# A 7x7 depthwise convolution on one core: two image rows to a partition at loading, odd rows moved by ScalarE

## The chip, the core and the metric

One core of a Trainium2 chip runs the whole program. Its engines work side by side, each through its own queue in order: TensorE (PE in the profile; PEld is its weight load), VectorE (DVE), ScalarE (ACT), GpSimd (POOL) and SyncE (SP), which here only issues DMA transfers. SP and ACT both issue DMAs. Engines and DMAs wait for each other through semaphores. The metric is the device time of one execution in microseconds (us); lower is better. Before the change the median of 14 runs is 9291.06 us (9283.38 to 9296.27).

## What is computed

Two layers work on a tensor x of 32 images, 128 channels and 56 x 56 pixels, all in float32. The first is a depthwise 7x7 convolution, then a layer norm, a mixture of experts and a residual sum; the second is a per-token attention and a second, softly routed mixture. The change touches only the convolution:

```python
def _forward(input, dw_kernel, dw_bias, ...):      # input: (32, 128, 56, 56)
    x = jax.lax.conv_general_dilated(
        input, dw_kernel, (1, 1), ((3, 3), (3, 3)),
        feature_group_count=C, dimension_numbers=('NCHW', 'OIHW', 'NCHW')
    ) + dw_bias[None, :, None, None]
    x = jnp.transpose(x, (0, 2, 3, 1))             # layer norm, router, experts follow
    ...
```

So every channel has its own 7x7 filter, and each of its 32 images is filtered with a border of three zeros.

## The kernel before

The convolution runs as matmuls over image rows. A loop of 64 steps (`for c in range(CH)`) treats two channels at once: channel c on partitions 0 to 63, the "half" r = 0, and channel c + 64 on partitions 64 to 127, the half r = 1. Image row h of a channel lies on partition r*64 + h, so 56 of each half's 64 partitions are used. A partition holds that row of all 32 images, each with three zeros on both sides (`xin`, 32 x 62 numbers). The filter enters as a band matrix (`band`, one DMA per half), which DVE turns over into `br` with its output columns sorted into even and odd rows (L265); a POOL instruction (L269) adds some bands. `xs` (L273, POOL) holds the sums of neighbouring pixels.

`products(c, part)` (L226 to L249) makes three kinds of products: part 0, "evens", from every other pixel of `xin` with 4 taps; part 1, "odds", the same with 3 taps; part 2, "boths", from `xs` with 4 taps. For each tap and each half it issues four matmuls, one for each pair of 16 images (b) and row parity (i). The four lie on four column strips of the PE array, and the half chooses the rows of the array, as `tile_position=(r * HP, q)` says. I call these four a block. One step has 8 + 6 + 8 = 22 blocks, 88 matmuls; a float32 matmul leaves two records in the profile, so a step has 176. The text issues the blocks of the two halves in turn.

After the products, for each half r: ACT copies the evens from PSUM to `ea` (L281); DVE makes the even pixels of the result (`ot`, L285, twice), then evens out of boths (L289), then the odd pixels (L294, twice); ACT issues two DMAs that write `ot` to `conv_d` (L299). `xin`, `band` and `br` have three buffers each, filled in turn; the PSUM pool has eight banks, of which a step takes six.

What a reader sees as one loop is spread over the queues by a scheduler when the program is built: it places each instruction on its engine's queue by what it takes to be the earliest time, so that the queue order is not the order of the text. In the program before, the blocks of the halves alternate through all 64 steps, and ACT's queue runs, from step 1 on, in pairs of steps: `ea` of two steps (four copies), then the eight write DMAs of the two. Each DMA also takes one of eight semaphores in rotation, and waits until the DMA that had it last has landed.

After the loop a router stage begins with small constants (`gam`, `wg`, `bet`, `bgt`, `raw`, `jm`, `jl`) and the reading back of `conv_d` (`ct`). In the program before, the loads of `gam`, `wg` and `bgt` and most work on `raw`, `jm` and `jl` stand early in the convolution.

Of the kernel before, what the change touches and what calls it, by code (L numbers as in the profile page):

```python
# [8 lines left out]
F32 = mybir.dt.float32  # L9
# [3 lines left out]
ALU = mybir.AluOpType  # L13
# [4 lines left out]
P = 128  # L18
GJ = 7
GT = P * GJ  # L20
KS = 7
PAD = 3
# [3 lines left out]
def conv_attn_hybrid_kernel(  # L26
# [24 lines left out]
    nc = tc.nc  # L51
    N, C, H, W = x.shape
# [34 lines left out]
    band_d = dram.tile([C, KS * 2 * H], F32, name="band_d")  # L87
# [106 lines left out]
    WP = W + 2 * PAD  # L194
    HP = P // 2
    NB = N // 2
    WH, CH = W // 2, C // 2
    NE, NO = (KS + 1) // 2, KS // 2
    BL = (KS - 1) * 2 * H + H
    HH, QP = H // 2, P // 4  # L200
    assert H <= HP and N % 2 == 0 and W % 2 == 0 and NB * (WH + 1) * 4 <= 2048
    assert H % 2 == 0 and HH <= QP
    with tc.tile_pool(name="cv_c", bufs=1) as cc, tc.tile_pool(
        name="cv", bufs=3
    ) as cv, tc.tile_pool(name="cv_p", bufs=8, space=PSUM) as cvp:
        wt = cc.tile([C, KS, KS], F32, name="wt")
        nc.sync.dma_start(wt.rearrange("c a b -> c (a b)"), dw_kernel.rearrange("c o a b -> c (o a b)"))
        gp = cc.tile([C, KS, 2 * H], F32, name="gp")
        nc.vector.memset(gp, 0.0)
        for kh in range(KS):  # L210
            nc.vector.tensor_copy(gp[:, :, H - 1 - PAD + kh], wt[:, kh, :])
        nc.sync.dma_start(band_d, gp.rearrange("c a b -> c (a b)"))
        bias = cc.tile([P, C], F32, name="bias")
        nc.sync.dma_start(bias, dw_bias.partition_broadcast(P))

        nbuf = 3
        bands = [cc.tile([P, KS, 2 * H], F32, name=f"band{i}") for i in range(nbuf)]
        turned_bands = [cc.tile([P, KS + NO, 2, QP], F32, name=f"br{i}") for i in range(nbuf)]
        xins = [cc.tile([P, N, WP], F32, name=f"xin{i}") for i in range(nbuf)]
        for i in range(nbuf):  # L220
            nc.vector.memset(bands[i], 0.0)
            nc.vector.memset(turned_bands[i], 0.0)
            nc.gpsimd.memset(xins[i], 0.0)
        cview = conv_d.rearrange("n c (h w) -> c h n w", w=2 * W)

        def products(c, part):  # L226

            bt, xi, xs = turned_bands[c % nbuf], xins[c % nbuf], sums_of_x[c]
            wide = WH + (part == 1)
            pss = [cvp.tile([P, NB, wide], F32, name="cps") for r in range(2)]  # L230
            taps = NO if part == 1 else NE
            for a in range(taps):
                for r in range(2):
                    rows = slice(r * HP, r * HP + H)
                    for b in range(2):
                        imgs = slice(b * NB, (b + 1) * NB)
                        if part < 2:
                            at_ = 2 * a + part
                            w_, m_ = at_, xi[rows, imgs, at_ : at_ + 2 * wide - 1 : 2]
                        else:  # L240
                            w_, m_ = (0, KS, KS + 1, KS + 2)[a], xs[rows, imgs, a : a + WH]
                        for i in range(2):
                            q = i * HP + b * QP
                            nc.tensor.matmul(  # L244
                                pss[r][q : q + QP], bt[rows, w_, i, :], m_,
                                start=(a == 0), stop=(a == taps - 1),
                                tile_position=(r * HP, q), skip_group_check=True,
                            )
            return pss  # L249

        sums_of_x = {}
        for c in range(CH):
            bt, br, xi = bands[c % nbuf], turned_bands[c % nbuf], xins[c % nbuf]
            for r in range(2):
                rows, cr = slice(r * HP, r * HP + H), r * CH + c
                nc.sync.dma_start(
                    bt[rows].rearrange("p a b -> p (a b)")[:, :BL],
                    bass.AP(
                        band_d.tensor, band_d.offset + cr * KS * 2 * H, [[1, H], [1, BL]]
                    ),  # L260
                )
                nc.sync.dma_start(
                    xi[rows, :, PAD : PAD + W], x[:, cr].rearrange("n h w -> h n w")
                )
            nc.vector.tensor_copy(  # L265
                br[:, :KS, :, :HH],
                bt[:, :, :H][:, :, ::-1].rearrange("p k (h i) -> p k i h", i=2),
            )
            nc.gpsimd.tensor_tensor(  # L269
                br[:, KS:, :, :HH], br[:, 2:KS:2, :, :HH], br[:, 1 : KS - 1 : 2, :, :HH], ALU.add  # L270
            )
            xs = sums_of_x[c] = cv.tile([P, N, WP // 2], F32, name="xs")
            nc.gpsimd.tensor_tensor(xs, xi[:, :, 0::2], xi[:, :, 1::2], ALU.add)  # L273
            evens = products(c, 0)
            odds = products(c, 1)
            boths = products(c, 2)
            ot = cv.tile([P, NB, 2, W], F32, name="ot", bufs=3)
            for r in range(2):
                cr = r * CH + c
                ea = cv.tile([P, NB, WH], F32, name="ea", bufs=4)  # L280
                nc.scalar.copy(ea, evens[r])  # L281
                mine = slice(r * HP, (r + 1) * HP)
                for i in range(2):
                    of = slice(i * HP, (i + 1) * HP)
                    nc.vector.scalar_tensor_tensor(  # L285
                        ot[mine, :, i, 0::2], odds[r][of, :, :WH], bias[of, cr : cr + 1], ea[of],
                        ALU.add, ALU.add,
                    )
                nc.vector.scalar_tensor_tensor(  # L289
                    ea, boths[r], bias[:, cr : cr + 1], ea, ALU.add, ALU.subtract  # L290
                )
                for i in range(2):
                    of = slice(i * HP, (i + 1) * HP)
                    nc.vector.tensor_tensor(  # L294
                        ot[mine, :, i, 1::2], ea[of], odds[r][of, :, 1:], ALU.subtract
                    )
                for b in range(2):
                    q = r * HP + b * QP
                    nc.scalar.dma_start(  # L299
                        cview[cr][:, b * NB : (b + 1) * NB, :],  # L300
                        ot[q : q + HH].rearrange("p n i w -> p n (i w)"),
                    )
# [96 lines left out]
    with tc.tile_pool(name="rt_c", bufs=1) as cc, tc.tile_pool(  # L399
        name="rt", bufs=6  # L400
# [170 lines left out]
        loaded, c = 0, 0  # L571
# [16 lines left out]
    with tc.tile_pool(name="sel", bufs=1) as se, tc.tile_pool(  # L588
        name="sel2", bufs=2
# [260 lines left out]
    with tc.tile_pool(name="sc_c", bufs=1) as cc, tc.tile_pool(  # L850
        name="sc", bufs=4
# [181 lines left out]
    with tc.tile_pool(name="ex_w", bufs=2) as ew, tc.tile_pool(  # L1033
        name="ex", bufs=3
# [72 lines left out]
        for i, (e, b) in enumerate(blocks):  # L1107
            n = GR if b < NBIG else GR // NQ
# [112 lines left out]
    with tc.tile_pool(name="at_c", bufs=1) as cc, tc.tile_pool(  # L1221
        name="at", bufs=2
# [524 lines left out]
        while k < NT or work or choosing or choices:  # L1747
# [15 lines left out]
            if k == NT // 2 + 3:  # L1763
                rows = at.tile([E2, FF2], F32, name="hbr", tag="zr", bufs=1)
# [16 lines left out]
    with tc.tile_pool(name="f_c", bufs=1) as cc, tc.tile_pool(  # L1781
        name="f", bufs=2
    ) as fp, tc.tile_pool(name="f_p", bufs=1, space=PSUM) as fps, tc.tile_pool(
        name="o", bufs=2
# [21 lines left out]
        for i in range(NS):  # L1806
# [11 lines left out]
            h = fp.tile([P, FF2], F32, name="fh")  # L1818
# [107 lines left out]
```

## Time and profile before

| | us |
|---|---|
| median of 14 runs | 9291.06 |
| the profiled execution, whole | 9286.61 |
| its span (first to last instruction) | 9284.9 |
| first matmul of the convolution | 12.96 |
| end of its last matmuls | 600.2 |
| PE busy in 100 to 600 us | 499.3 of 500 |
| ACT busy in 100 to 600 us | 55.3 of 500 |

The span is what one execution shows between its first and last instruction; the whole time has 1.7 us more around it. Rows of a timeline give the start, the time and the engine, then the source line, the operation, what is written and read, and how many instructions were merged into the row; in brackets stands the idle time before the first of them and what ended it. Here 56*32 beside a matmul is the part of the array it uses, and 56x448 the moving operand. A busy share close to 1 on PE does not show by itself that PE sets the pace, since the ends of its matmuls are modelled.

### The profile page before, as it was taken

The numbers are of one execution on the slowest core, as the hardware profiler recorded it, in microseconds if no ns is written. First come the engines' busy times: TensorE is split into PE (matmuls) and PEld (weight loads), VectorE is DVE, ScalarE is ACT, GpSimd is POOL, SyncE is SP. The second block draws the span as 40 slices with busy tenths as digits, with TensorE's granted clock in tenths as the row PEclk, the third lists the DMA queues.
The fourth block names the chain that finished last, engine by engine and source line by source line (L and its number), as shares of the span: only waits on it lengthen the run. The fifth ranks groups of instructions, "written<-read, shape, count | busy, mean of one in ns | idle before, by whom it ended". The sixth has DMA issues, their size and how long they took to land. (4 is left out here: it accounts for less than half of the span.)

```text
span 9284.9 us, 169079 instructions
## 1 busy us (share of the span) xinstructions
PE 8369.2 (90%) x64986; PEld 6988.8 (75%) x64986; DVE 6611.2 (71%) x9050; ACT 5297.9 (57%) x13301; POOL 7025.1 (76%) x4996
## 2 busy tenths in 40 slices
PE   9996667776999999996999999999999999999988
PEld 5776455554777777775889999999999999999744
DVE  7879766675222222225999999999999999999623
ACT  1138322232333333334888888888888888888600
POOL 2235466665888888888999999999999999999500
PEclk9998788888999999998999999999999999999855
DMA  9984255564444444442000000000000000000299
GB/s 205 219 212 151 84 161 170 172 176 142 74 73 74 68 73 71 68 71 32 25 31 29 32 32 32 25 32 32 29 32 32 25 32 32 29 31 32 87 313 328
DMA packets 865534, 828.22 MB, mean 89 GB/s; under 512 B 403162, under 2 KB 756829, under 8 KB 845628
## 3 DMA queue, kind: packets, MB, share of 16 engines
q1 hardware_dynamic: 457818, 472.35, 18.0%
q0 software_dynamic: 177664, 188.81, 11.5%
q10 hardware_dynamic: 229248, 156.26, 5.7%
q8 instruction: 515, 8.44, 0.4%
q14 instruction: 289, 2.37, 0.1%
HBM read 464.45 MB, written 353.64 MB: 88 GB/s over the span
## 5 line engine op out<-in xcount | busy, mean ns | idle before, releaser
L161 POOL TENSOR_TENSOR s<-s,q 128x2048 f32<-128x2048 f32 x784 | 3600.7, 4610 | 54.8 <-DVE s L161 30.3
L161 DVE TENSOR_TENSOR s<-kv,c 128x2048 f32<-128x2048 f32 x784 | 1787.1, 2279 | 22.3 <-POOL c L161 19.9
L161 POOL DMA_INDIRECT t_d<-ys,xe x992 | 1543.1, 1556 | 330.3 <-issue 285.2
L161 DVE TENSOR_TENSOR ev<-s,kv 128x2048 f32<-128x2048 f32 x784 | 1783.6, 2275 | 1.0 <-ACT s L161 1.0
L161 ACT ACTIVATE s<-s 128x2048 f32<-128x2048 f32 x784 | 1506.0, 1921 | 467.7 <-POOL s L161 464.2
L161 PE MATMUL sm<-ident,s 128*128 128x128 f32 x12544 | 1521.6, 275 | 72.8 <-DVE oT L161 65.1
L161 PE MATMUL sm<-ident,ev 128*128 128x128 f32 x12544 | 1518.5, 275 | 1.8 <-DVE ev L161 1.8
L161 PEld LDWEIGHTS sm<-ident,s 128*128 128x128 f32 x12544 | 1395.6, 142 | 95.3 <-issue 74.8
L161 PEld LDWEIGHTS sm<-ident,ev 128*128 128x128 f32 x12544 | 1427.3, 143 | 46.7 <-DVE ev L161 3.8
L1132 ACT ACTIVATE hT<-ph,b1t 128x512 f32<-128x512 f32 (+1 forms) x992 | 680.1, 686 | 1128.1 <-PE ph L161 1120.6
L1149 DVE TENSOR_TENSOR ys<-py,b2t 128x512 f32<-128x512 f32 (+1 forms) x248 | 171.5, 692 | 1400.5 <-PE py L161 1304.3
L863 POOL DMA_INDIRECT xb_d<-xs,rd x784 | 768.9, 981 | 484.0 <-issue 205.7
L161 PEld LDWEIGHTS py<-w,hT 128*128 128x128 f32 x7936 | 924.1, 191 | 116.9 <-issue 64.0
L161 PE MATMUL py<-w,hT 128*128 128x128 f32 x7936 | 925.3, 275 | 0.0
L161 PE MATMUL ph<-xeT,w 128*128 128x512 f32 (+1 forms) x1984 | 905.6, 600 | 0.0
L161 PEld LDWEIGHTS ph<-xeT,w 128*128 128x128 f32 x1984 | 364.8, 194 | 363.3 <-issue 359.7
L161 ACT COPY add<-px 128x512 f32<-128x512 f32 x224 | 116.1, 533 | 843.2 <-remote 514.6
L161 DVE SCALAR_TENSOR_TENSOR xs<-pa,rst,add 128x256 f32<-128x256 f32 x784 | 331.2, 478 | 338.7 <-remote 108.8
L161 PE MATMUL pa<-rw,ct 128*128 128x256 f32 x1568 | 410.3, 411 | 142.8 <-DVE xs L161 88.2
L161 PEld LDWEIGHTS pa<-rw,ct 128*128 128x128 f32 x1568 | 323.7, 210 | 266.5 <-issue 139.1
L161 PE MATMUL kv<-wq,zT 128*128 128x256 f32 x1568 | 418.0, 390 | 57.5 <-DVE ev L161 57.4
L244 PE MATMUL cps<-xin,br 56*32 56x448 f32 (+1 forms) x7168 | 441.0, 584 | 16.5 <-DVE br L265 13.0
(354 smaller groups left out, 13779.7 us busy)
## 6 DMA issues: line engine op xcount, KB each, us to landing
ct<-conv_d SPq DMA_DIRECT2D x192, 448.0 KB
xin<-in_x_dram SPq DMA_DIRECT2D x128, 392.0 KB
conv_d<-ot ACTq DMA_DIRECT2D x256, 196.0 KB
t_d<-xs ACTq DMA_DIRECT2D x112, 448.0 KB
tr<-t_d SPq DMA_DIRECT2D x112, 448.0 KB
out_dram<-oo ACTq DMA_DIRECT2D x32, 1568.0 KB
to<-t_d SPq DMA_DIRECT2D x30, 1568.0 KB
xg<-in_x_dram SPq DMA_DIRECT2D x96, 448.0 KB
```

The costliest lines, as they stand in the source:

```text
L161: r = getattr(self.engine, name)(*a, **k)
L244: nc.tensor.matmul(pss[r][q : q + QP], bt[rows, w_, i, :], m_, start=(a == 0), stop=(a == taps - 1), tile_position=(r * HP, q), skip_group ...
L863: s = nc.gpsimd.indirect_dma_start(out=xb_d, out_offset=bass.IndirectOffsetOnAxis(ap=idx, axis=0), in_=row, in_offset=None, bounds_check=R ...
L1132: nc.scalar.activation(hT[:, f, :, :rows], ph[:, :, :rows], AF.Gelu, bias=b1t[:, f : f + 1])
L1149: nc.vector.tensor_tensor(ys[:rows], py[:rows], across(b2t, SB)[:rows], ALU.add)
```

## The change

The shape of the load changes. Two consecutive image rows of a channel are contiguous in DRAM, so that one descriptor can carry 112 numbers instead of 56. Row pair p of a half now arrives on partition r*64 + p (28 partitions, 448 bytes a piece); ACT then copies the second row of each pair to partition r*64 + 32 + p, so that even image rows lie on partitions 0 to 27 of a half and odd rows on 32 to 59. `xin` grows from 32 x 62 to 32 x 118 numbers on a partition, as the odd row needs a place beside the even one. The load overwrites the right border, so POOL clears it again in every step (new L274). The band matrix is split alike, even and odd rows by a DMA each: four band DMAs in a step where there were two. The matmuls take all 64 partitions of a half, with zeros in the unused ones. Line numbers after L250 move by up to ten.

```diff
-        xins = [cc.tile([P, N, WP], F32, name=f"xin{i}") for i in range(nbuf)]
+        xins = [cc.tile([P, N, WP + W], F32, name=f"xin{i}") for i in range(nbuf)]
...
-                    rows = slice(r * HP, r * HP + H)
+                    rows = slice(r * HP, (r + 1) * HP)
...
             for r in range(2):
-                rows, cr = slice(r * HP, r * HP + H), r * CH + c
+                cr = r * CH + c
+                for i in range(2):
+                    q = r * HP + i * QP
+                    nc.sync.dma_start(
+                        bt[q : q + HH].rearrange("p a b -> p (a b)")[:, :BL],
+                        bass.AP(
+                            band_d.tensor, band_d.offset + cr * KS * 2 * H + i,
+                            [[2, HH], [1, BL]],
+                        ),
+                    )
+                q = r * HP
                 nc.sync.dma_start(
-                    bt[rows].rearrange("p a b -> p (a b)")[:, :BL],
-                    bass.AP(
-                        band_d.tensor, band_d.offset + cr * KS * 2 * H, [[1, H], [1, BL]]
-                    ),
-                )
-                nc.sync.dma_start(
-                    xi[rows, :, PAD : PAD + W], x[:, cr].rearrange("n h w -> h n w")
-                )
+                    xi[q : q + HH, :, PAD : PAD + 2 * W],
+                    x[:, cr].rearrange("n (h i) w -> h n (i w)", i=2),
+                )
+                nc.scalar.copy(
+                    xi[q + QP : q + QP + HH, :, PAD : PAD + W],
+                    xi[q : q + HH, :, PAD + W : PAD + 2 * W],
+                )
+            nc.gpsimd.memset(xi[:, :, PAD + W : WP], 0.0)
...
-            nc.gpsimd.tensor_tensor(xs, xi[:, :, 0::2], xi[:, :, 1::2], ALU.add)
+            nc.gpsimd.tensor_tensor(xs, xi[:, :, 0:WP:2], xi[:, :, 1:WP:2], ALU.add)
```

The scheduler also builds other queues from this text. What stands in them is part of the program as built:

- ACT, from step 5 on in most steps: `ea` of step c (two copies), the copy of half 1 of step c+1, the copy of half 0 of step c+2, the four write DMAs of step c. At steps 28, 34, 40, 46, 52 and 58 it is `ea`, then both halves of c+1 and half 0 of c+2.
- PE: the evens of 40 of the 64 steps (1, 6 to 26, 30 to 32, 36 to 38, 42 to 44, 48 to 50, 54 to 56, 60 to 62) no longer alternate. Three blocks of half 0 stand in a row, then three of half 1, then the fourth of each, which waits for POOL's clearing. Odds and boths alternate as before, and so do the evens of the other 24 steps.
- SP: two band DMAs more in each step, and the loads of `gam`, `wg`, `bgt` and `bet` stand behind the convolution; so does the work on `raw`, `jm` and `jl`.

## The prediction

> **What bounds the kernel now.** I read the stage table first (busy time by 100 us), then the weight loads of single steps, then who waits in 100 to 560 us, then ACT and DVE at the stage's end.
>
> ```profile
> 100.00:200.00 100.00, 100.00 (x1972) 65.79 (x1964) 83.41 (x128) 10.53 (x21) 26.19 (x22) 1.00 1.05 220
> 200.00:300.00 100.00, 100.00 (x1975) 58.10 (x1967) 78.18 (x121) 11.94 (x24) 26.09 (x22) 1.00 1.05 217
> 300.00:400.00 100.00, 100.00 (x1983) 72.84 (x1975) 81.62 (x126) 10.18 (x20) 26.18 (x23) 1.00 1.05 219
> 400.00:500.00 100.00, 100.00 (x1978) 91.81 (x1969) 80.09 (x123) 11.75 (x24) 27.92 (x23) 1.00 1.02 218
> ```
>
> The columns are PE, PEld, DVE, ACT, POOL, the granted clock, the DMA share, GB/s. PE and the DMAs both look full. The counts decide: 7908 matmul records in 400 us, at 176 a step, are 8.90 us a step, the same in each row.
>
> ```profile
> 301.45 0.10 PEld L244 LDWEIGHTS cps<-xin,br 56*32 56x32 f32 x1 [0.15 <-issue]
> 301.45 0.10 PEld L244 LDWEIGHTS cps<-xs,br 56*32 56x32 f32 x1
> ...
> 301.80 0.12 PEld L244 LDWEIGHTS cps<-xin,br 56*32 56x32 f32 x2
> 301.83 0.14 PEld L244 LDWEIGHTS cps<-xs,br 56*32 56x32 f32 x2
> 301.87 0.11 PEld L244 LDWEIGHTS cps<-xin,br 56*32 56x32 f32 x2
> 301.93 0.12 PEld L244 LDWEIGHTS cps<-xs,br 56*32 56x32 f32 x2
> 302.21 0.22 PEld L244 LDWEIGHTS cps<-xin,br 56*32 56x32 f32 x8 [0.16 <-DVE ot L294]
> 302.58 0.23 PEld L244 LDWEIGHTS cps<-xin,br 56*32 56x32 f32 x8 [0.16 <-issue]
> 303.00 0.23 PEld L244 LDWEIGHTS cps<-xin,br 56*32 56x32 f32 x8 [0.19 <-issue]
> ...
> 306.36 0.23 PEld L244 LDWEIGHTS cps<-xin,br 56*32 56x32 f32 x8 [0.19 <-issue]
> ```
>
> Eight records start every 0.42 us (302.58 to 306.36: nine slots in 3.78 us); for boths it is 0.38 (20.44 to 22.72 us: six slots). 14 x 0.42 + 8 x 0.38 = 8.92 us, the whole step: PE never waits, it is the pace. The slots at 301.45 and 301.80 show what a slot is: four records of the last block of boths, half 1 (`xs`), beside four of the first block of evens, half 0 (`xin`). A block thus takes two slots (each float32 matmul passes twice), and a slot is full only because the other half has a block running.
>
> ```profile
> POOL xs L273 <- DMA xin<-in_x_dram: 190.9, 35, 7.5
> ACT ea L281 <- DMA xin<-in_x_dram: 148.7, 10, 15.7
> DVE ot L285 <- ACT ea L281: 71.3, 25, 4.7
> ```
>
> Who waits for loads is POOL and ACT (us, times, longest); on PE and PEld this list has no DMA. So lighter DMAs have nothing to shorten here, but ACT, late without harm so far, will now stand before PE.
>
> **The reordered evens.** The change doesn't touch `products`, but its copies move the evens' blocks on PE's queue: in 40 of 64 steps three blocks of half 0 stand in a row before three of half 1. A second block of one half cannot share slots with the first. By slots: alternating, the fourth block of half 0 begins in slot 6. In the new order half 0 takes slots 0 to 5 alone, half 1 is reached when the third block's second pass is issued (slot 5) and takes 5 to 10, and the fourth block of half 0 begins in slot 10. Four slots lost, 4 x 0.42 = 1.68 us. No alternation was broken before, so the trace has no such stall. Bounds: 0, if the idle half can be fed from further down the queue, and five slots, 2.10 us, if half 1 begins one slot later. I take 1.68, by the nearest row, four column strips of one row group alone in the final stage:
>
> ```profile
> 8823.79 1.06 PE L1814 MATMUL p_fh<-fw,pTb 128*32 128x512 f32 x8
> ```
>
> Eight records, one block, 1.06 us with its drain; the shortest single record there is 0.592, so two passes of some 0.47 behind each other. Step 1 waits for its copy anyway: 39 x 1.68 = **65.5 us** (0 to 82).
>
> The Trainium skill, "TensorEngine Tiling (Array Packing)", Key Properties, says that tiles operate independently and can execute weight loads and matmuls in parallel. The mixed slots agree. Taken alone it would make the new order free, and the sum 10. "TensorE: Matmul & The Clock Gate", Step-by-step, says that the matmuls themselves stay in program order and only weight loads are pulled ahead. That speaks against this change and gives the sum below; no run here shows it yet.
>
> **ACT's copies.** 128 copies of 28 x 1792. Rows: 536 ns for 448 numbers (L281), 1921 for 2048 (`s<-s`), so 0.866 ns a number, 536 + 1344 x 0.866 = 1.70 us; at most 1.92 by the longer row. ACT gets 3.4 us a step on top of 1.0 for `ea` and four DMA issues of 0.31. The wait counts, not the sum:
>
> ```profile
> 576.80 3.15 ACTq L299 DMA_DIRECT2D conv_d<-ot  x4
> 579.99 0.97 ACT L281 COPY ea<-cps 128x448 f32<-128x448 f32 x2 [11.69 <-DMA conv_d<-ot]
> 599.58 0.68 DVE L289 SCALAR_TENSOR_TENSOR ea<-cps,bias,ea 128x448 f32<-128x448 f32 x1 [0.84 <-PE cps L244]
> ```
>
> Let T be the start of a step's evens (590.25 in the last). DVE can combine boths of half 0 at T+9.33 (599.58), and ends the step 4.70 us later (L289, L285, two L294, L289, two L294: 582.69 to 587.39), at 14.03. ACT goes on 1.21 later (DVE done at 578.78, `ea` at 579.99): it is held by the write DMAs in front. `ea` 0.97, copy 1.70, 0.1 to wake PE: T+18.0. That copy is half 1 of two steps on, due in its slot 2: 2 x 8.92 + 0.84 = 18.7. So 0.7 us are left in 8.92 us steps, and 4 in slowed ones: nothing for the usual step. With both halves behind `ea` (six places) the copy ends at 19.7: 1.0 us each, 6 us. Steps 3 to 5 are queued like that in a row: two steps take 18.9, 0.5 us a step, 2 us. In step 1 the second copy stands behind the writes of step 0: by the same sum from the first steps' times it ends near 30.7 us, 7 us late, plus 1.5 for slow slots after an idle PE (before: 0.75 instead of 0.38 at 51.08 to 53.32, after a stall). Against that the kernel before also loses there: 1484 records by 100 us are worth 75 us of the 87 since the start, 12 lost, 3 of them the slow first slots. Together 0 (-5 to +9).
>
> **DMAs.** `xin` has half the packets, the bytes are unchanged. In 100 to 560 us q1 spends 65.1% of 16 engines on 191947 packets (25 ns each, mostly 224 bytes), q10 38.3% on 94780 (30 ns, 448 bytes). At 30 ns the 1792 packets a step need 3.4 us of 16 engines instead of 5.6. PE, full at 1.05 share, hides that. SP's queue: six issues of some 0.35 where there were four, 2.1 us in 8.9, hidden. But ten DMAs now share eight semaphores a step, so a load waits for the writes of a step before. Half 1's load for step c+3 needs the first writes of step c landed: it can issue some 8.4 us into step c+1, and its copy comes 16.2 us into it (`ea` of step c+2); landing took about 8 us under full load (issue 301.9, POOL released 310.07). It just holds in steps of 8.92 us and has room in longer ones, so I cost it nothing; if the cover goes, 1 us a step.
>
> **The rest.** POOL's clearing is 96 numbers; memsets of 128 take 0.2 us, POOL is 27% busy, and only the fourth block waits for it. The three first memsets grow 1.75 to 3.3 us, behind the band's round trip. Zero rows add no columns. Behind the loop the router's constants are now loaded after five `ct` transfers; their nearest row is `bet`, issued 610.67, its matmul at 616.06. I take 2 us (0 to 5).
>
> **Sum:** 65.5 + 6 + 2 + 0 + 2 = 75.5 us. 9286.61 + 75.5 = 9362 in the profiled execution; the median is 4.45 above that, so **9367 us**, +0.8%. Below 0.2% (18.6 us) this kernel can't be told from no change.
>
> **Rivals.**
> - *The halves overlap all the same* (15%). For it: a mixed slot shows them independent. Against: all of them come from alternating blocks. Without the 65.5: 9301, from 9290 to 9315, "same" or a little slower.
> - *Loads or copies come late every step* (12%). For it: eight semaphores for ten DMAs, 0.7 us of room on ACT. Against: cheaper packets, longer steps. One more microsecond in 64 steps: 9367 + 64 = 9431.
> - *DMA is the limit after all, and lighter loads free PE* (3%), the other side. For it: a share of 1.05. Against: no DMA in PE's waits. Its price is what PE loses now: 12.96 to 600.2 is 587.2, less 64 x 8.90 is 17.6 us, so 9273 at best, and it needs the reordering free and ACT never late.
>
> **How the numbers follow.** My case, 70%: 9340 to 9395 (1.3 to 2.1 us a slowed step, plus the rest). The range for 8 in 10 takes in most of the overlapping halves' case and the first half of late loads: 9308 to 9425. Faster by over 0.2%: 0.03; within: 0.11 (most of the first rival); slower: 0.86.
>
> **What would show it.** Right: slowed steps at about 10.6 us between `xs` rows, others near 8.9; weight loads four, not eight, in a slot during the first blocks of those evens; PE's records a 100 us falling from 1975 to some 1700, at clock 1.00; `xin` waits on POOL shorter. Wrong: alternating and slowed steps equally long, or PEld waiting for `xin` or for the copy in most steps.

## The result, and the profile after

The changed kernel takes 9385.08 us (9379.09 to 9388.48) where the kernel before takes 9292.99 us (9281.88 to 9306.61) beside it: the ratio is 1.01, interval 1.009 to 1.011, some 92 us slower. The profiled execution has a span of 9371.6 us, 86.7 more than before. The convolution runs from 14.16 to 684.9 us where it ran from 12.96 to 600.2, so 84.7 of the 86.7 us lie at its end, and 2.0 behind it.

The stage table of the changed kernel, the same columns as in the prediction (PE, PEld, DVE, ACT, POOL, granted clock, DMA share, GB/s):

```profile
100.00:200.00 100.00, 97.56 (x1769) 63.93 (x1764) 69.98 (x108) 43.94 (x40) 26.04 (x30) 1.00 0.92 196
200.00:300.00 100.00, 93.73 (x1626) 51.63 (x1618) 65.63 (x102) 42.54 (x39) 25.44 (x29) 0.97 0.88 183
300.00:400.00 100.00, 95.75 (x1728) 59.49 (x1723) 71.42 (x110) 41.82 (x37) 23.99 (x28) 0.98 0.92 190
```

PE's records fall from 1975 to some 1700 in 100 us, as forecast, and the DMA share falls below 1. The granted clock, 1.00 in these rows of the kernel before, is 0.97 and 0.98 in two of them. The busy column hides most of it (94 to 98%), so single steps have to be measured. A step's length is here the time from the first evens' matmul of one step to that of the next:

| steps | kernel before | changed |
|---|---|---|
| 24 reordered steps without a stall (6 to 14, 21 to 23, 26, ...) | 8.9 to 9.3, steps 6 and 56 10.9 and 10.6 | 9.23, mean |
| 1 | 8.93 | 17.23 |
| 3, 4 | 12.04, 13.34 | 11.44, 11.41 |
| 15 to 20 | 8.92 to 8.97 | 11.2 to 16.4, 21 us lost together |
| 24, 25 | 8.9 | 11.3, 10.5 |
| 28, 34, 40, 46, 52, 58 and 29, 35, 41, 47, 53, 59 | 8.9 to 9.1 | 9.7 to 10.6 |
| 30, 36, 37, 42, 48, 54, 60 | 8.9 to 9.2 | 11.0 to 16.4, 37 us lost together |

So the loss is not spread over the 40 reordered steps. It sits in stalls, and the profile shows what a stall is. PEld in the changed kernel in step 30:

```profile
330.82 0.17 PEld L244 LDWEIGHTS cps<-xin,br 64*32 64x32 f32 x4 [0.26 <-issue]
331.23 0.18 PEld L244 LDWEIGHTS cps<-xin,br 64*32 64x32 f32 x4 [0.24 <-issue]
334.47 0.15 PEld L244 LDWEIGHTS cps<-xin,br 64*32 64x32 f32 x8 [3.06 <-ACT xin L270]
335.03 0.22 PEld L244 LDWEIGHTS cps<-xin,br 64*32 64x32 f32 x4 [0.41 <-issue]
335.78 0.26 PEld L244 LDWEIGHTS cps<-xin,br 64*32 64x32 f32 x12 [0.52 <-issue]
```

Half 0 runs alone (four loads to a slot) until its three blocks are through; then PEld stands for 3.06 us until ScalarE's copy of half 1 is there, and the slots after that take 0.75 us (335.03 to 335.78) instead of 0.42. The stage table over just that stretch (columns as above):

```profile
335.00:338.00 3.00, 3.00 (x32) 1.15 (x32) 2.86 (x6) 1.17 (x1) 1.63 (x1) 0.50 1.04 182
```

The granted clock is 0.50 there, and a slot takes 1.8 times as long. Over the whole convolution the clock is 0.97, where the kernel before has 0.99: of 671 and 587 us that is some 20 and 6 us, so that, as an estimate, some 14 us of the loss are the slower clock after stalls.

Why is the copy late? ACT's queue before it, in the same kernel:

```profile
325.60 2.32 ACTq L309 DMA_DIRECT2D conv_d<-ot  x3
...
331.36 0.31 ACTq L309 DMA_DIRECT2D conv_d<-ot  x1
331.71 0.97 ACT L291 COPY ea<-cps 128x448 f32<-128x448 f32 x2 [8.65 <-DMA conv_d<-ot]
332.70 3.47 ACT L270 COPY xin<-xin 28x1792 f32<-28x1792 f32 x2
```

Four write DMAs of step 28, two `ea` of step 29, then the copy (332.70, 1.73 us: done at about 334.4, and PEld goes on at 334.47). Three writes leave by 327.92, and DVE has finished step 28 at 327.58; the fourth leaves only at 331.36. In the trace each transfer names its semaphore: the fourth write has the one that the first write of the same step took at 325.60, and that one's last piece landed 0.02 us before the fourth write was issued. With ten transfers a step on eight semaphores, the rotation gave the same semaphore to two of the four writes of one step. The load queue waits in the same way. SP's waits, 100 to 560 us, in the changed kernel:

```profile
SPq L258 <- DMA conv_d<-ot: 160.8, 56, 7.9
SPq L258 <- DMA xin<-in_x_dram: 73.6, 34, 3.5
SPq L266 <- DMA conv_d<-ot: 64.0, 40, 5.5
SPq L266 <- PE cps L244: 11.9, 4, 4.2
```

and in the kernel before:

```profile
SPq L262 <- PE cps L244: 179.4, 96, 6.5
SPq L256 <- DVE ea L289: 98.5, 27, 4.5
```

Before, SP waits for what it must wait for, the buffers that PE and DVE still read. After, it waits for writes of `conv_d`, with which a load has nothing to do but the semaphore. The bands then come late, and for the first time others wait for them. Waits of the changed kernel in 100 to 560 us:

```profile
DVE br L275 <- DMA band<-band_d: 52.8, 21, 6.2
...
PEld cps L244 <- ACT xin L270: 36.9, 23, 4.9
PE cps L244 <- ACT xin L270: 19.5, 16, 4.0
```

Steps 15 to 19 show this alone. No write is held between 60 and 228 us, yet each of these steps loses 2.3 to 3.8 us, 13.5 us together. DVE at the start of this stretch:

```profile
169.91 0.56 DVE L275 COPY br<-band 128x392 f32<-128x392 f32 x1 [6.25 <-DMA band<-band_d]
```

The band had landed at 169.79, and `br` of the next four steps (181.21, 193.91, 205.58, 216.85 us) follow their band's landing by 0.1 to 0.5 us too. Each of these five band loads had left its queue only when its semaphore came free, 3.6 to 7.6 us after the instruction ahead of it. A late band makes DVE late, DVE the writes, and the writes `ea` and the copies behind them. The larger stalls, in steps 20, 30, 36, 37, 42, 48, 54 and 60, each have in addition a write that was held for 1.5 to 4 us shortly before.

The waits on such semaphores can be counted from the trace: an issue that leaves its queue more than 0.3 us after the instruction ahead of it (the queue's own waiting instructions left out), and within 0.12 us of the last landing on its own semaphore. The table holds the kernels of the experiments too; the sums are us of the queue's time over the convolution, in brackets the number. The whole time since the instruction ahead is counted, so that a wait for a buffer in it is counted too.

| kernel | loads held (SP) | writes held (ACT) | start of first to start of last matmul |
|---|---|---|---|
| before | 3 (2) | 138 (83) | 586.7 |
| changed | 452 (174) | 51 (18) | 670.2 |
| only the order of the evens | 3 (1) | 150 (81) | 594.1 |
| before, ten DMAs | 56 (45) | 290 (134) | 643.9 |
| changed, copies on GpSimd | 467 (218) | 5 (3) | 669.2 |
| changed, two bands by GpSimd | 138 (57) | 38 (28) | 609.7 |
| changed, odd band by copy | 118 (46) | 28 (22) | 613.2 |
| changed, copies first | 363 (194) | 52 (26) | 630.3 |
| odd band by copy, copies first | 24 (15) | 4 (4) | 583.0 |

In the kernel before ACT's writes are held too, 132 of the 138 us by the landing of a load that had the semaphore, and it costs next to nothing: only `ea` stands behind them, and PEld waits for it 3.3 us in 100 to 600 us. In the changed kernel it is the other way round: 345 of the 452 us are loads that a write held up.

### The profile page after: what moved, and what is told of

The parts are those of the page before. It is cut to its first block, busy times and chain, and to the rows that moved or that the text cites. A ratio compares the mean times of both kernels' runs of the same rounds, so it can differ in the third digit from the quotient of the medians.

```text
span 9371.6 us, 169605 instructions
## 1 busy us (share of the span) xinstructions
PE 8423.0 (90%) x64986; PEld 7000.7 (75%) x64986; DVE 6607.4 (71%) x9050; ACT 5520.0 (59%) x13429; POOL 7041.8 (75%) x5060
## 5 line engine op out<-in xcount | busy, mean ns | idle before, releaser
L244 PE MATMUL cps<-xin,br 64*32 64x448 f32 (+1 forms) x7168 | 514.4, 604 | 48.0 <-ACT xin L270 32.3
```

The lines of the kernel that those rows point to most:

```text
L244: nc.tensor.matmul(pss[r][q : q + QP], bt[rows, w_, i, :], m_, start=(a == 0), stop=(a == taps - 1), tile_position=(r * HP, q), skip_group ...
```

## The experiments

Ten runs on three more chips. The kernel before takes 9071 us beside the first four, 9069 beside the next three and 9310 beside the last three, so each run is read against the kernel before on its own chip. Times in the first four expectations are meant for the chip of the result, where it takes about 9291 us: what counts is the difference from that.

**Only the order of the evens**, in the kernel before:

```diff
-            for a in range(taps):
-                for r in range(2):
+            blocks = [(a, r) for a in range(taps) for r in range(2)]
+            if part == 0:
+                blocks = [(a, r) for r in range(2) for a in range(3)] + [(3, 0), (3, 1)]
+            for a, r in blocks:
```

> The kernel before with nothing changed but the order of the evens' blocks: three taps of half 0, three of half 1, then the last of each, in all 64 steps. Theory R: 64 x 1.68 = 108 us, 9400, steps of 10.6 us, weight loads four to a slot in those blocks. If the halves overlap although they stand in blocks of three (as the undisturbed reordered steps of the changed kernel, 9.0 to 9.25 us, let one think): 64 x 0 to 0.3 us, 9293 to 9312.

Measured: 9076.74 against 9071.36 us, ratio 1.0004 (0.9995 to 1.0014), 5.4 us in 64 steps (-5 to +13), 0.08 us a step. Its stage table:

```profile
300.00:400.00 100.00, 100.00 (x1944) 83.37 (x1934) 79.21 (x122) 11.56 (x23) 25.64 (x21) 1.00 1.03 212
```

1944 records in 100 us are 9.05 us a step. The matmul starts of step 32's evens and odds show why: in groups of four, they begin at 0, 0.56, 0.98, 1.39, 1.41, 1.82, 1.85, 2.23, 2.26 us. From the fourth group on they come in pairs, so half 1 runs beside half 0 although six groups of half 0 stand ahead of it in the queue. (The records don't name the half; that two groups of one half don't run side by side is seen at 330.82 above, where half 0 alone has four loads to a slot.) The odds, which can be told by their form, begin at 3.36 us, while evens, all of which stand ahead of them in the queue, begin until 4.38 us. In the first two slots the boths of the step before still run beside the evens, so that only the third slot is half empty. Half a slot is 0.21 us, an estimate of what the order can cost. The prediction's 108 us for this run are not there.

**The band of a half in one transfer**, in the changed kernel, to come back to eight DMAs (`band_d` also gets one more row of the band for each channel):

```diff
-                for i in range(2):
-                    q = r * HP + i * QP
-                    nc.sync.dma_start(
-                        bt[q : q + HH].rearrange("p a b -> p (a b)")[:, :BL],
...
-                            [[2, HH], [1, BL]],
+                nc.sync.dma_start(
+                    bt[r * HP : (r + 1) * HP].rearrange("p a b -> p (a b)")[:, :BL],
...
+                        [[1, 2], [2, QP], [1, BL]],
```

> The band of a half comes by one DMA of 64 rows instead of two of 28 (source rows in the order even, odd), so a step issues eight DMAs on the eight semaphores, as before the change; ScalarE's copies stay. The scheduler puts 24 steps into the order of three blocks of a half in a row (40 in the changed kernel) and ScalarE's copies at other places of its queue. Theory S (loads wait for writes, because ten DMAs share eight semaphores, so the bands come late, VectorE is late, the writes and with them ScalarE's copies are late): SP waits for PE again and not for conv_d, VectorE waits less than 10 us for bands in 100 to 600 us (58 in the changed kernel), convolution steps of 9.0 to 9.3 us, 9295 to 9325 us. Theory Q (the copies stand behind the writes in ScalarE's own queue, whatever the loads do): the same stalls of 1 to 7 us at single steps, 9350 to 9410. The prediction's theory R (1.68 us for every reordered step): 24 steps, 40 us, 9330 to 9345, with reordered steps of 10.6 us.

Measured: 9411.64 against 9071.36 us, ratio 1.0375 (1.0359 to 1.0391): 340 us over before, far worse than any theory said. A row of the stage table and one of the waits in 100 to 560 us:

```profile
200.00:300.00 100.00, 76.40 (x1116) 28.52 (x1124) 47.43 (x74) 26.55 (x24) 16.43 (x20) 0.81 0.60 135
```

```profile
DVE br L273 <- DMA band<-band_d: 126.4, 16, 14.6
```

The DMA engines are busy for 0.60 of the time and yet the bands are late. The loads' queue has packets of four bytes that close a transfer: 14.1 for a transfer of 28 rows in the changed kernel, but 1.9 for this band (1022 packets in 100 to 560 us, less 14 for each of 64 `xin` transfers, over 65 bands). If each engine that takes part sends one, which no view names, a band of 64 rows was drained by two of sixteen engines. The run says nothing on the semaphores, since it put a slow transfer in their place.

**The copies on GpSimd** (`nc.scalar.copy` for the odd rows becomes `nc.gpsimd.tensor_copy`), ten DMAs as in the changed kernel:

> The changed kernel with the two copies of a step on GpSimd; the four band DMAs stay, ten DMAs a step on eight semaphores. ScalarE's queue is then what it was before the change (ea, then the writes), and 63 steps have three blocks of a half in a row. Theory Q: the stalls go, steps of 8.9 to 9.2 us, 9285 to 9320. Theory S: the loads still wait for the writes; bands and x are late in the same way and PE waits for them or for GpSimd's copy: 9340 to 9400. Theory R: 62 more steps of 1.68 us, 104 us, 9390 to 9410.

Measured: 9155.13 us, ratio 1.0093 (1.0078 to 1.0109), 84 us slower than before, inside theory S's range: nothing is gained by freeing ScalarE of the copies while the loads are held (467 us in the table above). 63 reordered steps instead of 40 do not make it slower either. It isn't a clean test of the queue: the scheduler also put ACT's writes between the two `ea` of a step at a few places, and steps 23, 32, 40, 49 and 57 take 15 us.

**Both of these edits:**

> Both edits together: eight DMAs a step, copies on GpSimd; some 36 steps reordered. Theories S and Q alike: 9280 to 9310, with steps of 8.9 to 9.1 us. If only the sum of both edits takes the stalls away, this run is near before while each alone is not. Theory R: 36 x 1.68 = 60 us, 9350.

Measured: 9374.42 us, ratio 1.0333 (1.0319 to 1.0347), 303 us over before. The band has the same shape here, and DVE waits 178.6 us for bands in 100 to 560 us, so this run says nothing on the two theories either.

**Ten DMAs in the kernel before.** Each band DMA cut in two, nothing else:

```diff
-                nc.sync.dma_start(
-                    bt[rows].rearrange("p a b -> p (a b)")[:, :BL],
...
+                for i in range(2):
+                    q = r * HP + i * HH
+                    nc.sync.dma_start(
+                        bt[q : q + HH].rearrange("p a b -> p (a b)")[:, :BL],
...
```

> The kernel before with one edit: each band DMA of 56 rows cut into two of 28 rows; the same bytes and packets, no copies, x as before. A step issues ten DMAs on the eight semaphores instead of eight. Theory S (a load now waits for a write of an earlier step that happens to hold its semaphore): SP waits for conv_d (no such wait before), the band and x loads come late, single steps stall by 1 to 7 us; +50 to +120 us over before. If the ten DMAs are harmless (the prediction's 0): within 10 us of before, and the changed kernel's loss must come from the copies or from the split x loads.

Measured: 9117.33 against 9069.4 us, ratio 1.0052 (1.0037 to 1.0068): 48 us from two more transfers a step that move no more data, just under the +50 to +120 that theory S gave. The place is not quite the one that was expected. ACT's queue and PEld at a stall of this run, and PEld's wait in 100 to 560 us:

```profile
233.07 15.18 ACTq L302 DMA_DIRECT2D conv_d<-ot  x8
248.29 1.84 ACT L284 COPY ea<-cps 128x448 f32<-128x448 f32 x4 [19.04 <-DMA conv_d<-ot]
```

```profile
245.49 0.21 PEld L244 LDWEIGHTS cps<-xin,br 56*32 56x32 f32 x4 [0.20 <-issue]
248.87 0.15 PEld L244 LDWEIGHTS cps<-xin,br 56*32 56x32 f32 x8 [3.18 <-ACT ea L284]
```

```profile
PEld cps L244 <- ACT ea L284: 40.7, 36, 3.9
```

DVE had finished the two steps at 240.6; the eight writes take until 248.25, seven of them issued within 0.1 us of the landing of the transfer that had their semaphore. Behind them stands `ea`, which empties PSUM, and PEld waits 3.18 us for that. Here it is mainly the writes that are held (290 us against 138), hardly the loads (56).

**Two of the four bands issued by GpSimd**, in the changed kernel, which leaves eight transfers a step in the rotation of SP and ACT, all of their old shape:

```diff
-                    nc.sync.dma_start(
+                    (nc.gpsimd if i else nc.sync).dma_start(
                         bt[q : q + HH].rearrange("p a b -> p (a b)")[:, :BL],
```

> The changed kernel; the two band DMAs of the odd rows are issued by GpSimd, which leaves eight a step on the semaphores that SP and ScalarE share; copies stay on ScalarE. Every transfer has the shape it has in the changed kernel. Theory S: SP's waits for conv_d go, stalls go, 0 to +25 us over before. If the shape of the loads or ScalarE's copies cost the time: +60 to +100 us over before, as the changed kernel.

Measured: 9107.15 us, ratio 1.0038 (1.0025 to 1.0051), 38 us over before; the changed kernel stands at 1.009. That lies between the two ranges: half of the loss and more goes with the same ten transfers and ScalarE's copies still there, but not all of it. 7.5 us are a later start (first matmul at 20.47 us, 12.96 before).

**The odd rows' band by a copy**, in the changed kernel. The odd rows' band is the even rows' band one number further on, so GpSimd makes it from that, and its two DMAs go:

```diff
+                nc.sync.dma_start(
+                    bt[r * HP : r * HP + HH].rearrange("p a b -> p (a b)")[:, : BL + 1],
...
+            for r in range(2):
+                q = r * HP
+                nc.gpsimd.tensor_copy(
+                    br[q + QP : q + HP, :KS, :, :HH],
+                    bt[q : q + QP, :, 1 : H + 1][:, :, ::-1].rearrange("p k (h i) -> p k i h", i=2),
+                )
```

> The changed kernel with the odd rows' band not loaded: it is the even rows' band one number further on, so the two band DMAs of 28 rows bring 729 numbers a row, and GpSimd fills the odd partitions of br from the even ones (two copies of 28 rows a step); VectorE's copy covers 96 partitions. Eight DMAs a step, half the band's bytes. Theory S: SP's waits for conv_d go, steps of 8.9 to 9.2 us, 0 to +25 us over before. If copies on ScalarE cost the time by themselves: +60 us and more, with PEld waiting for ScalarE's copy.

Measured: 9093.11 us, ratio 1.0025 (1.0016 to 1.0034), 24 us over before. SP waits for PE again above all, and for writes 17.5 us (225 in the changed kernel), but still 45 us for `x` loads:

```profile
SPq L264 <- PE cps L244: 252.8, 74, 7.9
SPq L256 <- DMA xin<-in_x_dram: 45.0, 27, 2.8
SPq L256 <- DMA conv_d<-ot: 15.1, 7, 6.8
```

Of what is left, step 1 has 9.3 us (18.18 us long: its second copy stands behind the writes of step 0), step 16 5.5, the start 3.7, and some fifteen steps 0.7 to 2.2 us each. 22 steps are still reordered.

**The same, with ScalarE's queue written out by hand.** In the changed kernel and in the last one, `ea`, `ea`, the two copies for two steps on, then the four writes, in each step; the loads of step c+2 stand in the text of step c. So half 1's copy for a step now stands ahead of the writes of two steps before, where it stood behind them:

```diff
+        act = InOrder(nc.scalar)
...
         for c in range(CH):
+            if c + 2 < CH:
+                load(c + 2)
...
+            for r in range(2):
+                act.copy(eas[r], evens[r])
+            if c + 2 < CH:
+                odd_rows(c + 2)
...
-                    nc.scalar.dma_start(
+                    act.dma_start(
```

The changed kernel beside them on their chip:

> The changed kernel itself, unedited, beside the other two on their chip. All theories: the loss seen at first, +80 to +95 us over before (ratio 1.009 to 1.011).

Measured: 9397.17 against 9309.97 us, ratio 1.0094 (1.0078 to 1.0109).

> The changed kernel with ScalarE's queue written out by hand: in every step ea, ea, the two copies for two steps on, then the four writes; the loads as they are, ten DMAs a step on eight semaphores. The copies no longer stand behind a write of their step. Theory Q (the copies' place behind the writes is what costs): the stalls for the copy go, 0 to +25 us over before. Theory S (the semaphores): writes still wait for loads to land, ea and the copies of the next step stand behind them and loads wait for writes: +40 to +80 us.

Measured: 9357.33 us, ratio 1.0044 (1.0029 to 1.0059), 47 us over before. The copies stall PE no more, but its loads are still held for 363 us, and the waits in 100 to 560 us show who is late instead: DVE, for its bands, and PE for DVE, which empties PSUM.

```profile
PEld cps L244 <- DVE ot L322: 40.1, 41, 1.8
DVE br L272 <- DMA band<-band_d: 39.6, 19, 5.9
```

> Both cures: the odd rows' band by GpSimd's copies (eight DMAs a step, as in the run that took the loss to +24 us) and ScalarE's queue written out by hand. Theories S and Q together: what was left of the loss (the copy behind the writes in step 1 and some 15 stalls of about 1 us) goes, -10 to +12 us against before. If something else is left (clock after a stall, GpSimd's extra copies): +20 us and more.

Measured: 9306.57 against 9309.97 us, ratio 0.9996 (0.9987 to 1.0005): the whole loss is gone. Two rows of its stage table:

```profile
200.00:300.00 100.00, 100.00 (x1973) 88.70 (x1964) 79.81 (x123) 48.95 (x44) 41.49 (x56) 1.00 0.91 200
300.00:400.00 100.00, 99.81 (x1961) 79.82 (x1956) 78.86 (x122) 48.97 (x44) 41.05 (x56) 1.00 0.88 198
```

PE has its 1960 to 1975 records again, with ACT 49% busy, and the granted clock is 1.00: the copies as such cost nothing that can be measured here. The two cures together:

| | half 1's copy behind the writes of two steps before | ahead of them |
|---|---|---|
| ten DMAs a step | 1.0094 (+87 us) | 1.0044 (+47 us) |
| eight DMAs a step | 1.0025 (+24 us) | 0.9996 (-3 us) |

Each takes away a part, and both are needed. The columns differ in two more things: writing out ACT's queue also let the scheduler alternate the evens in all steps but two, which by the first experiment is worth some 0.1 us a step, and the loads and DVE's `br` stand two steps earlier in the text. No run changed the number of semaphores with all else kept; the run with two bands issued by GpSimd comes nearest. No version was found that beats the kernel before by more than the measurement is uncertain.

## Why the prediction was right or wrong

The time was right, 9367 forecast and 9385 measured, and the size of the whole as well (75.5 us; 92 by the medians, 86.7 in the profiled execution). That was luck: the main step, 65.5 of the 75.5 us, was wrong, and what filled its place, at about the same size, is a step that the prediction had costed at nothing.

- **The reordered evens, 65.5 us: wrong.** The step that failed is "the fourth block of half 0 begins in slot 10". It took for granted that the queue reaches half 1 only when half 0's three blocks are issued. The run with nothing but that order measured 5.4 us for 64 steps; half 1 began in the fourth slot, not the sixth. The lag of half 1 by three slots is carried along, not lost: half 0's next blocks run beside half 1's late ones. In the changed kernel, 24 reordered steps without a stall took 9.23 us, 0.25 over an alternating one without (8.98). Why half 1 starts just there stays open. The Trainium skill, "TensorEngine Tiling (Array Packing)", Key Properties, had it that tiles run weight loads and matmuls in parallel, and this run agrees. Its "TensorE: Matmul & The Clock Gate", Step-by-step, keeps the matmuls in program order; the starts in the trace, with half 1 beside half 0 from the fourth group of six on, do not show such an order between the halves. The prediction weighed the two and followed the second.
- **Ten DMAs on eight semaphores, 0 us, "if the cover goes, 1 us a step": wrong, and the larger part of the loss.** Two more transfers alone cost the kernel before 48 us; taking them out of the changed kernel brought it from 1.0094 to 1.0025 or 1.0038. The prediction followed one load back to the writes of the step before and found that it "just holds". It did not follow the writes: a write too waits for its semaphore, and in the changed kernel `ea` and the copies stand behind it on ACT. A sign of it stood in its own list: `ACT ea L281 <- DMA xin<-in_x_dram: 148.7` was read as ACT waiting for loads, but `ea` reads only PSUM; what waited were the writes ahead of it, 132 us by the count above.
- **ACT's copies, 8 us: the mechanism right, the size not.** A copy took 1.73 us (1.70 forecast). The six places with both halves behind `ea` cost 1.0 us each (steps 29, 35, 41, 47, 53 and 59 lose 5.9 us together), as worked out. Steps 28, 34, 40, 46, 52 and 58 lose 6.6 us more; their copies stand behind the `ea` of two steps in a row. Not seen was the step after each, 30, 36 and 37, 42, 48, 54 and 60, with 37 us together: there the copy stands behind writes that are held, and six of these steps run partly at the clock of 0.50. "So 0.7 us are left in 8.92 us steps" was counted with writes that leave as soon as DVE is done.
- **The first steps, 0 (-5 to +9): inside the bounds.** Step 1 lost 8.3 us, as forecast (7 plus 1.5), and steps 3 to 6 lost less than before (5.1 against 9.5). Steps 0 to 6 and the start together came out 6 us longer than before.
- **Lighter DMAs, hidden: right, but they are less light than forecast.** In the changed kernel a 448-byte packet of `xin` took 40 ns, where 30 was taken from the writes of the same size. 1792 of them are 4.5 us of sixteen engines a step, against 4.9 us for 3584 packets of 22 ns before. In the last run, with eight transfers a step and no loss, it took 33 ns, which is 3.7 us a step. Nothing was gained by it: PE's pace there is that of the kernel before.
- **The rest, 2 us: not confirmed.** 86.7 less 84.7 is 2.0, but the first matmul behind the convolution, that of `bet`, comes 0.5 us later against its end than before (16.3 and 15.8 us), and what follows moves by -6 to +2 us between the two executions.
- **The rivals.** Two of them came true together: the halves overlap (9301), and loads and copies come late, not in every step, but by more than a microsecond a step on average (+64 forecast). 9301 + 64 is 9365. The prediction had set them against each other as alternatives, each with its own time, and so named the sum only by accident.
- **What would show it.** "Slowed steps at about 10.6 us" looks confirmed if one takes means: 10.86 us for the 40 reordered steps, 9.82 for the others. The list of single steps refutes it: 24 of the 40 are near 9.2, and 16 at 10.4 to 17.2. Four weight loads alone in a slot show for one slot of an undisturbed step, and for longer only while the copy is missing. PE's records did fall to some 1700, but not at clock 1.00. PEld waiting for the copy, which was named as a sign against the prediction if it came in most steps, was there 23 times in some 44 steps.

What stays open: how the changed kernel's loss divides between held loads and held writes. Steps 15 to 19 give 13.5 us to held loads alone; in the larger stalls both come together, and the runs took both away at once. With the copies first, held loads and writes still cost 47 us, and there PE waits for the bands by way of DVE; in the kernel before with ten DMAs it was mainly the writes.

## What to carry to other kernels

Count the transfers of a loop's step against the semaphores that they share: with exactly as many transfers a step as semaphores, writes waited for loads here, off PE's path; two more transfers made loads and writes wait for each other without any data between them, on it (48 us for no data more). An instruction on a critical path should not stand close behind a DMA issue on the same queue; if the scheduler puts it there, write the queue out by hand and put the instruction ahead, or a step earlier. And read step lengths one by one: a mean over a class of steps can agree with a theory that no single step follows.

## What the runs showed of the hardware that was not expected

- Matmuls of one row half start beside those of the other although three blocks of the other stand ahead of them: 0.08 us a step for the new order, in a run of 64 such steps.
- A band whose outermost dimension is two (two times 32 rows) closed with 1.9 small packets a transfer, one of 28 rows with 14.1, and the kernel was 3.8% slower than before where the changed kernel is 0.9 to 1.0% slower. The Trainium skill, "DMA: Bandwidth & Descriptors", Rules for kernel authors, says that an outermost dimension of fewer than 16 confines the transfer to at most that many engines; the 1.9 closing packets a transfer agree.
- What a packet of one size takes depends on the run: 448 bytes of `xin` took 40 ns in the changed kernel and 33 ns in the last run, beside 31 and 32 ns for the writes; a band's packets of 2912 bytes took 131 ns before and 184 ns in the changed kernel. Half as many packets of twice the bytes (22 ns for 224 before) saved 8% and 25% of the DMA time of `x`.
- After PEld had stood for 3.06 us in step 30, PE's slots took 0.75 us instead of 0.42 from 335.03 to 338.02, and the step lost 5.2 us (14.17 against 8.93). The granted clock of those 100 us was 0.98, so the mean hides it; from 335 to 338 it was 0.50. In the changed kernel's convolution a gap of 2.06 us between two matmul starts (up to 406.3 us) was followed by such a stretch of 3.41 us.
